# Spreading the column logits of a graph-attention layer without TensorE transposes, and ranking six last batches ahead instead of four

**Chip, cores, metric.** One core of one Trainium2 chip. The metric is the device time of one execution in microseconds (us); lower is better.

## The reference, cut to what matters

128 independent graphs of 128 nodes and 512 features go through four residual layers, each followed by a layernorm. All is float32. The change touches the attention of layer 1 alone:

```python
h = einsum('bnc,cf->bnf', x, W)
s1 = h @ a1                                   # one number for each node (row logit)
s2 = h @ a2                                   # one number for each node (column logit)
e  = leaky_relu(s1[:, :, None] + s2[:, None, :], 0.2) * adj
att = softmax(e, axis=2)
x  = layernorm(x + elu(att @ h + beta * h))   # ... layers 0, 2 and 3 cut
```

Rows of `e` lie on partitions. So `s1` is a scalar of each partition, but `s2` has to stand as a row of 128 numbers on *every* partition. It is computed as a column, one number on each partition. How it gets from column to row is the subject.

## The kernel before

The kernel writes each batch as a generator ("chain") that asks for engines. A small planner runs all chains, orders the requests by when it reckons they can start, then by rank, and so records one fixed order of instructions for each engine. The reckoned durations decide only the order; on the chip every engine runs its list strictly in that order.

```python
def use(self, engine, work, take=None, late=0.05, urgent=False): ...
    # work: time reckoned on the engine; late: from its end until the result is there

def at(self, r):                               # when a request could start, by the plan
    engine, _, take, _, _ = r["want"]
    t = max(r["ready"] + (MARGIN if engine == "PE" else 0.0), self.free.get(engine, 0.0))
    ...
def run(self):
    ...  # takes the request with the least (at, not urgent, rank, n)
         # self.now = r["ready"] = t + work + late
```

`MARGIN` is 1.0 us and is given to TensorE's requests alone. The attention, for a group of two batches:

```python
def attention1(gr, h):
    yield gr.logits[h]
    ...
    b0 = yield use("PE", 0.3, "tr", late=0.2, urgent=True)
    p = bank([P, 2, P], "tr")
    for i in range(2):
        nc.tensor.transpose(p[:, i, :], s[:, 2 * h + i, 1:2].to_broadcast([P, P]), ident)
    be = yield use("DVE", 2.1, "e", urgent=True)
    z = one.tile([P, 2, P], F32, name="z")
    for i in range(2):
        nc.vector.tensor_scalar(z..., p..., s[:, 2 * h + i, 0:1], None, op0=ALU.add)
    give(b0)
    e = buf([P, 2, P], "e")
    nc.vector.scalar_tensor_tensor(e, z, ALPHA, z, op0=ALU.mult, op1=ALU.max)
    ...  # times adj, maximum; exponentials on ScalarE; normalise, block turn
    yield use("SP", 0.1, late=2.0)
    to_rows(et..., scratch)                    # e_d <- et, and then eT <- e_d
    ...
# main: the last four batches rank 16 places ahead (in group() too)
for i in range(NB):
    plan.start(batch(i), i if i < NB - 4 else i - 16)
plan.run()
```

A transpose of a column broadcast along its free axis gives the row on every partition, in PSUM, in one step.

## Time and profile before

| | before |
|---|---|
| median (first three runs) | 3364.07 us (3363.28 to 3366.58) |
| profiled span | 3366.0 us |
| TensorE busy | 3324.6 us, 99% |
| VectorE busy | 2669.9 us, 79% |
| transposes of `s` | 128 records, source line 383 |
| TensorE's waits over 0.15 us, 20 to 3200 us | 9.5 us in all |
| the same from 3200 us to its last product | 16.5 us in all |

The last two rows are summed from TensorE's timeline, which gives the idle time before each group in brackets. I call these stretches "the middle" and "the end" below. The program is bound by TensorE nearly everywhere; the one large hole is near the end. The lines that carry this stand in the prediction.

How to read the names in profile lines: `out<-in` are tiles. `mm`, `tr` and `sc` are TensorE's results in PSUM. `x` is a batch, `xT` the batch turned for the query-key products of layer 3. `e`, `et` and `eT` are the attention matrix of layer 1, its block turn, and the turned copy that TensorE reads; `pr`, `pt` and `prT` are the same for layer 3. `scr` is the work tile of the products that make the logits `s`; names in `_d` are scratch in DRAM.

### The profile page before, as it was taken

The numbers are of one execution on the slowest core, as the hardware profiler recorded it, in microseconds if no ns is written. First come the engines' busy times: TensorE is split into PE (matmuls) and PEld (weight loads), VectorE is DVE, ScalarE is ACT, GpSimd is POOL, SyncE is SP. The second block draws the span as 40 slices with busy tenths as digits, with TensorE's granted clock in tenths as the row PEclk, the third lists the DMA queues.
The fourth block names the chain that finished last, engine by engine and source line by source line (L and its number), as shares of the span: only waits on it lengthen the run. The fifth ranks groups of instructions, "written<-read, shape, count | busy, mean of one in ns | idle before, by whom it ended". The sixth has DMA issues, their size and how long they took to land.

```text
span 3366.0 us, 43501 instructions
## 1 busy us (share of the span) xinstructions
PE 3324.6 (99%) x14729; PEld 2070.5 (62%) x14729; DVE 2669.9 (79%) x5527; ACT 1189.7 (35%) x3457; POOL 923.1 (27%) x1031
## 2 busy tenths in 40 slices
PE   9999999999999999999999999999999999999987
PEld 5665656566565666566656656665656665666655
DVE  7878786886978878877877886887887787788775
ACT  3433333333233334343333333333333333333332
POOL 2322221331322312312322331232232232232221
PEclk9999999999999999999999999999999999999999
DMA  4332323223232323222232322232322323232222
GB/s 157 98 103 63 104 75 93 69 80 113 68 99 76 97 79 91 94 79 82 79 109 66 100 85 91 85 89 83 91 85 82 98 73 97 76 94 88 69 82 75
DMA packets 458191, 296.01 MB, mean 88 GB/s; under 512 B 315888, under 2 KB 389744, under 8 KB 457968
## 3 DMA queue, kind: packets, MB, share of 16 engines
q1 hardware_dynamic: 457968, 293.23, 29.0%
q8 instruction: 117, 1.92, 0.2%
q14 instruction: 106, 0.87, 0.1%
HBM read 150.54 MB, written 142.61 MB: 87 GB/s over the span
## 4 chain that ended last, share of the span: by engine, by line
PE 90%; DVE 6%; DMA 2%; issue 1%; SPq 0%; ACT 0%; POOL 0%; POOLq 0%; DVEq 0%; ACTq 0%
PE mm L195 47%; PE mm L442 27%; PE tr L203 6%; PE sc L572 4%; PE tr L619 4%; PE mm L543 3%; DVE st L161 1%; DMA p_d<-pt 1%; DMA prT<-p_d 1%; DVE scr L516 1%; DVE x L648 1%; PE tr L383 0%; SPq L486 0%; DVE t L645 0%; DVE x L182 0%
## 5 line engine op out<-in xcount | busy, mean ns | idle before, releaser
L442 PE MATMUL mm<-xT,wqkv_sb 128*128 128x256 f32 x4096 | 918.2, 381 | 8.8 <-DVE st L161 8.8
L195 PE MATMUL mm<-w_sb,yT 128*128 128x512 f32 x2048 | 913.9, 596 | 2.3 <-ACT yT L206 2.3
L442 PEld LDWEIGHTS mm<-xT,wqkv_sb 128*128 128x128 f32 x4096 | 771.4, 190 | 138.3 <-issue 20.6
L168 POOL TENSOR_TENSOR rstd<-ve,neghalf 128x1 f32<-128x1 f32 x640 | 406.6, 635 | 1100.6 <-DVE ve L165 996.9
L195 PEld LDWEIGHTS mm<-w_sb,yT 128*128 128x128 f32 x2048 | 383.3, 191 | 453.3 <-issue 441.6
L188 POOL TENSOR_TENSOR x<-x,o 128x512 f32<-128x512 f32 x128 | 175.9, 1374 | 1128.3 <-DVE o L636 1117.6
L195 PE MATMUL mm<-wqkv_sb,xT 128*128 128x512 f32 x1024 | 464.4, 596 | 0.0
L195 PE MATMUL mm<-wproj_sb,oT 128*128 128x512 f32 x1024 | 460.9, 598 | 1.8 <-ACT oT L628 1.8
L590 ACT ACTIVATE pr<-pr,nmx 128x128 f32<-128x128 f32 x1024 | 397.6, 391 | 176.1 <-DVE nmx L586 174.6
L161 DVE BATCH_NORM_STATS2 st<-x 128x6 f32<-128x512 f32 x512 | 348.1, 680 | 3.1 <-ACT x L550 1.9
L579 DVE TENSOR_TENSOR pr<-sc,maskb 128x1024 f32<-128x1024 f32 x128 | 156.3, 1221 | 218.8 <-PE sc L572 218.0
L195 PEld LDWEIGHTS mm<-wproj_sb,oT 128*128 128x128 f32 x1024 | 191.8, 191 | 223.6 <-issue 214.4
L177 ACT ACTIVATE x<-x,nmr,rstd 128x512 f32<-128x512 f32 x256 | 205.0, 810 | 351.6 <-DVE nmr L175 326.9
L195 PEld LDWEIGHTS mm<-wqkv_sb,xT 128*128 128x128 f32 x1024 | 189.6, 190 | 199.0 <-issue 191.4
L206 ACT COPY yT<-tr 128x512 f32<-128x512 f32 x256 | 146.8, 582 | 263.9 <-PE tr L203 263.6
L188 POOL TENSOR_TENSOR x<-x,beta_sb 128x512 f32<-128x512 f32 x128 | 167.1, 1307 | 177.1 <-DVE xt L556 131.2
L516 DVE SCALAR_TENSOR_TENSOR scr<-x,wa_rows 128x512 f32<-128x512 f32 x256 | 200.4, 783 | 15.5 <-ACT x L177 10.2
L468 ACT COPY v<-mm 128x512 f32<-128x512 f32 x128 | 74.9, 585 | 347.7 <-PE mm L195 347.5
L450 ACT ACTIVATE qkT<-mm 128x512 f32<-128x512 f32 x128 | 76.1, 594 | 341.2 <-PE mm L442 341.0
L590 ACT ACTIVATION_READ_ACCUMULATOR pr<-pr,nmx 128x1 f32 x1024 | 193.1, 189 | 0.0
L188 POOL TENSOR_TENSOR x<-x,bias_sb 128x512 f32<-128x512 f32 x128 | 182.6, 1436 | 32.9 <-PE tr L203 22.9
L182 DVE TENSOR_SCALAR x<-x,mv,rstd 128x512 f32<-128x512 f32 x256 | 172.5, 676 | 14.4 <-POOL rstd L168 14.0
(63 smaller groups left out, 3558.6 us busy)
## 6 DMA issues: line engine op xcount, KB each, us to landing
p_d<-pt SPq DMA_DIRECT2D x128, 512.0 KB, 2.6
prT<-p_d SPq DMA_DIRECT2D x128, 512.0 KB, 3.8
x<-in_x SPq DMA_DIRECT2D x128, 256.0 KB, 2.9
x_d<-xt SPq DMA_DIRECT2D x128, 256.0 KB, 2.0
xT<-x_d SPq DMA_DIRECT2D x512, 64.0 KB, 2.5
out<-x SPq DMA_DIRECT2D x128, 256.0 KB, 2.0
e_d<-et SPq DMA_DIRECT2D x64, 128.0 KB, 1.7
eT<-e_d SPq DMA_DIRECT2D x64, 128.0 KB, 2.2
```

What stands on the lines that cost most here:

```text
L161: nc.vector.bn_stats(st, src)
L168: nc.gpsimd.tensor_tensor(rstd, ve, neghalf, op=ALU.pow)
L177: nc.scalar.activation(xb, xb, AF.Identity, bias=nmr, scale=rstd)
L182: nc.vector.tensor_scalar(xb, xb, mv[:, 0:1], rstd, op0=ALU.subtract, op1=ALU.mult)
L188: nc.gpsimd.tensor_tensor(dst, dst, other, op=ALU.add)
L195: nc.tensor.matmul(p, lhs(k), rhs(k), start=(k == 0), stop=(k == K - 1))
L203: nc.tensor.matmul(p[:, k, :], xb[:, k * P : (k + 1) * P], nodes, start=True, stop=True)
L206: nc.scalar.copy(yT, p)
L442: nc.tensor.matmul(p[:, j, :], wqkv_sb[:, k, (c + j) * P : (c + j + 1) * P], gr.xT[:, k, :], start=(k == 0), stop=(k == K - 1),)
L516: nc.vector.scalar_tensor_tensor(scr, xb, 1.0, wa_rows[:, j, :], op0=ALU.mult, op1=ALU.mult, accum_out=gr.s[:, b, j : j + 1],)
L579: nc.vector.tensor_tensor(pr, sc.rearrange("p j c m -> p (j c) m"), maskb[:, None, :].to_broadcast([P, H, P]), op=ALU.add,)
L590: nc.scalar.activation(pr[:, j, :], pr[:, j, :], AF.Exp, bias=nmx[:, j : j + 1], accum_out=sums[:, j : j + 1],)
```

## The change

The intent: TensorE is the bound, so take the 128 transposes from it. VectorE turns the column inside its 32x32 blocks, a 1 KB store writes the pieces to DRAM in node order, and a 128 KB load reads them back, the same row for every partition. Besides, six batches rank ahead instead of four, by 12 places instead of 16.

```diff
-        b0 = yield use("PE", 0.3, "tr", late=0.2, urgent=True)
-        p = bank([P, 2, P], "tr")
-        for i in range(2):
-            nc.tensor.transpose(p[:, i, :], s[:, 2 * h + i, 1:2].to_broadcast([P, P]), ident)
+        yield use("DVE", 0.2)
+        st = small.tile([P, 2, Q, S // Q], F32, name="s2")
+        nc.vector.transpose(
+            st.rearrange("p i c u -> p i u c"),
+            s[:, 2 * h : 2 * h + 2, 1:2, None].to_broadcast([P, 2, S // Q, Q]),
+        )
+        row = dram.tile([2 * Q, Q, S // Q], F32, name="s_d")
+        yield use("SP", 0.1, late=2.0)
+        nc.sync.dma_start(row..., st[::S]...)
+        bz = yield use("SP", 0.1, "z", late=2.2)
+        z = buf([P, 2, P], "z")
+        nc.sync.dma_start(z, row...[None, :].to_broadcast([P, 2 * P])...)
         be = yield use("DVE", 2.1, "e", urgent=True)
-        z = one.tile([P, 2, P], F32, name="z")
-        for i in range(2):
-            nc.vector.tensor_scalar(z..., p..., s[:, 2 * h + i, 0:1], None, op0=ALU.add)
-        give(b0)
+        nc.vector.tensor_tensor(
+            z, z, s[:, 2 * h : 2 * h + 2, 0:1].to_broadcast([P, 2, P]), op=ALU.add
+        )
         e = buf([P, 2, P], "e")
         nc.vector.scalar_tensor_tensor(e, z, ALPHA, z, op0=ALU.mult, op1=ALU.max)
+        give(bz)
...
-            plan.start(batch(i), i if i < NB - 4 else i - 16)
+            plan.start(batch(i), i if i < NB - 6 else i - 12)
```

(The ranks of `attention1` and `query_key` change in the same way. `z` gets two buffers.)

## The prediction

> **What bounds the kernel now.** I read the page first: the busy shares, then the chain that ended last. Both name TensorE.
>
> ```profile
> PE 3324.6 (99%) x14729; PEld 2070.5 (62%) x14729; DVE 2669.9 (79%) x5527; ACT 1189.7 (35%) x3457; POOL 923.1 (27%) x1031
> PEclk9999999999999999999999999999999999999999
> PE 90%; DVE 6%; DMA 2%; issue 1%; SPq 0%; ACT 0%; POOL 0%; POOLq 0%; DVEq 0%; ACTq 0%
> ```
>
> TensorE is busy 3324.6 of 3366.0 us, and its work is 90% of the chain. So only two things can shorten the span: less TensorE work, or fewer of the 41.4 us in which it idles. VectorE at 79% has room, and nothing that only it does counts unless TensorE waits for it.
>
> Then I looked for the idle time in the waits of TensorE alone:
>
> ```profile
> PE mm L442 <- DVE st L161: 8.8, 1, 8.8
> PE tr L619 <- DMA prT<-p_d: 7.9, 6, 6.0
> PE tr L383 <- DVE scr L516: 2.7, 4, 1.0
> PE tr L203 <- DMA eT<-e_d: 1.2, 1, 1.2
> ```
>
> The columns are microseconds in total, times, and the longest. One wait of 8.8 us is the largest; the second is one of 6.0 us and five small ones. The first transfers and the end of the program (the last matmul ends at 3356.9 of 3366.0, then VectorE and the store finish) make up most of the rest. Between 1000 and 3000 us the idle stretches I could find sum to only some 2 us. The timeline places the two long waits near the end:
>
> ```profile
> 3262.22 7.03 PE L195 MATMUL mm<-wproj_sb,oT 128*128 128x512 f32 x16
> 3278.04 16.80 PE L442 MATMUL mm<-xT,wqkv_sb 128*128 128x256 f32 x64 [8.79 <-DVE st L161]
> ...
> 3304.04 10.63 PE L442 MATMUL mm<-xT,wqkv_sb 128*128 128x256 f32 x48
> ...
> 3348.39 1.98 PE L619 MATMUL tr<-prT,v 128*64 128x128 f32 x16 [5.99 <-DMA prT<-p_d]
> ```
>
> The view blames a VectorE statistic for the 8.8 us, but that releaser is an inference. These products read xT; the last layer-2 product ended just before 3262.4, and after it come a maximum, an add, a layernorm, a block transpose and two steps of transfers. The four xT loads issued at 3273.42 took 2.55 us to issue and such a load lands in a median 2.5 us: that is the true releaser. There is a second loss: 64 records took 16.80 us here, though 48 took 10.63 us shortly after, which would be 14.2 us for 64. So 2.6 us more were lost to a slow clock after the pause.
>
> **What the Trainium skill says.** "TensorE: Matmul & The Clock Gate", Part 4 (PE-mode transpose), puts a transpose at about 275 ns inside a kernel. The trace agrees on duration (mean 281, median 273 ns), but duration is not what the engine loses: transposes are pipelined, and start to start tells the cost, below. The same page, Part 1 (the HAM clock gate), says that an idle window of some 3.4 us drops the clock to half; the trace agrees, both after the 8.79 us pause (above) and after the 5.99 us one (16 records in 1.98 us where the same group elsewhere takes 1.09). "DMA: Bandwidth & Descriptors", Anatomy of one DMA, gives about 2.0 us of fixed cost, mostly waiting for the write to be confirmed; the nearest transfers of this trace land in 1.7 us (store) and 2.2 us (load). "VectorE: DVE Perf Modes", The three transpose paths, says VectorE turns 32x32 blocks only, in 311 ns for 128x128; the trace has a mean of 311 ns for that shape. Hence blocks here need two transfers to become a row on every partition.
>
> **What the change removes.** 64 pairs of transposes (128 records). A pair costs what it delays its neighbours by:
>
> ```profile
> 1065.76 3.62 PE L442 MATMUL mm<-xT,wqkv_sb 128*128 128x256 f32 x16
> 1069.21 0.38 PE L383 MATMUL tr<-ident,s 128*128 128x128 f32 x2
> 1069.43 7.07 PE L442 MATMUL mm<-xT,wqkv_sb 128*128 128x256 f32 x32
> 1076.34 0.38 PE L383 MATMUL tr<-ident,s 128*128 128x128 f32 x2
> 1076.56 3.62 PE L442 MATMUL mm<-xT,wqkv_sb 128*128 128x256 f32 x16
> ```
>
> Start to start a pair takes 1069.43 - 1069.21 = 0.22 us, not 2 x 0.281. So 64 x 0.22 = 14.1 us of TensorE time go, all on the path, since TensorE runs gapless there. With them go TensorE's four direct waits for the logits, 2.7 us. These were transposes placed ahead of other work, just before VectorE had finished; I count them in full and keep an allowance below.
>
> **What it adds on VectorE.** Removed: the 128 adds that read the transposes from PSUM, 38.4 us in the rows by shape. Added: 64 block turns of 128x64. The trace has turns of 128 columns at 311 ns and of 512 at 702, so 1.02 ns a column, which gives an estimate of 0.25 us for 64: 16 us. And 64 adds of 128x256 SBUF operands; the like product with the adjacency takes 454 ns: 29.1 us. Sum 45 against 38.4: 7 us more on an engine with about 700 us free. No effect on the end.
>
> **What it adds in transfers.** 64 stores of 1 KB and 64 loads of 128 KB. By the nearest rows, the two together take some 0.3 + 1.7 + 0.4 + 2.2 = 4.6 us from turn to landing, against about one for the transposes. So a group's attention starts some 4 us later. This lies beside other work if the order is made for it: the recorded order of the new kernel places other products between. At the start, eleven batches of the first mix come ahead of the first product that needs attention in both orders, and one more layer-0 product now precedes it, so TensorE reaches it near 59.6 us (57.7 + 3.4 for the product - 0.6 for pairs - 0.9 for waits). I add up the new chain from the logits at 42.3 us: turn and add ahead of it 0.9, two transfers 4.6, four VectorE steps 1.8, exponentials 1.2, normalise and turn 2.0, two transfers 4.6: about 57.4 us. It fits by some 2 us.
>
> **What it moves.** The last six batches instead of four rank ahead, by 12 places instead of 16. In the old order, after the last layer-2 product only one pair of output projections is left to hide the road to xT: the 7.03 us group above, then the pause. In the new order there stand after it eight products of value mixing, two projections, eight more mixings, eight query-key products, eight mixings and two projections before the bulk of the last two groups' products. And the first of these groups seems to have its own layer-2 products over 40 us earlier (a group of 40 query-key products, some 17 us, stands between). So the 8.79 us pause and its 2.6 us of slow clock should go: 11.4 us. From the last 24 + 4 products of this stretch to the end the two orders are the same, so the 6.0 us wait for the last prT, its slow clock and the 9 us of finish should stay.
>
> **Sum.** 14.1 + 2.7 + 11.4 = 28.2 us. Against it an allowance of 3.2 us for new waits. It is a choice: SP issues in order and must wait 64 more times for a store to land before the load behind it, as it does today:
>
> ```profile
> SPq L216 <- DMA p_d<-pt: 258.2, 116, 4.5
> SPq L216 <- DMA e_d<-et: 69.3, 52, 2.1
> ```
>
> At the latter's 1.3 us a time that is some 85 us more of SP standing still, which can delay a prT behind it. Today TensorE's five short prT waits cost 1.9 us. Net 25 us: 3364.07 - 25 = **3339 us**, 0.74% faster, "same" at 2%.
>
> **The rivals.** (1) SP takes the place of TensorE's waits: the pairs of transfers stall loads of prT, xT and x, and TensorE waits a little in each of 64 groups. For it: SP's strict order, and five prT waits already at zero slack. Against it: SP waits over 600 us each for out and for pt to be produced, so it is mostly early. At 0.3 us a group this gives back 19 us: 3358. (2) The tail gap is not filled but moves, because the last groups still end their layer 2 together. For it: VectorE is dense near the end. Against it: the order above. It would leave only the transposes: 3348 to 3352. (3) VectorE becomes the bound where it is dense, in the first 60 us, and delays layer 0. The added 7 us over 3366 make this worth 2 us at most. (4) Everything works and the new order also trims the last prT wait and its cold products: 3331.
>
> **Range and chances.** The transposes are sure to within 1 us, the tail is a probable 11, the waits are open by some 10 either way. Low end: all of it plus a few us of the final wait, 3330. High end: the tail gain lost or SP costing some 15 us, 3353. To pass 2% would take 67 us, more than all idle time (41.4) and the transposes together (55.5), so faster has 0.01. Slower by 2% would need over 1 us of new wait per group: 0.01.
>
> **What would show it.** In the new profile: no transpose rows for s; TensorE's busy time near 3324.6 - 14.1 - 2.6 = 3308; no wait above 2 us of the query-key products near the end and the clock full until the last prT wait; that last wait still 4 to 8 us. The store lands in under 2.2 us, the load in under 2.6. VectorE's busy time rises by about 7 us. Waits for eT by TensorE stay under 3 us in all. I would be wrong if prT, eT or x waits in the middle sum to over 8 us (rival 1), if a pause of several us remains before query-key products near the end (rival 2), or if the first use of eT waits over 2 us.

## The result

| | before | after |
|---|---|---|
| median | 3365.32 us (4 runs) | 3353.43 us (3352.33 to 3360.93, 4 runs) |
| ratio | | 0.997 (0.9952 to 0.9987) |
| profiled span | 3366.0 us | 3351.8 us |
| TensorE's waits, middle / end | 9.5 / 16.5 us | 16.3 / 7.6 us |

12 us are gained by the medians, 0.35%, and 0.30% by the ratio. I had said 25, with 3330 us as the low end and 3353 as the high end; the median is just beyond the high end. The time is "same" at 2%, as forecast; the size is wrong by a factor of two.

First the page of the kernel after: busy time, and the chain that ended last.

```profile
PE 3312.7 (99%) x14601; PEld 2059.2 (61%) x14601; DVE 2664.7 (80%) x5527; ACT 1186.6 (35%) x3457; POOL 934.9 (28%) x1031
PE 85%; DVE 11%; DMA 3%; issue 1%; SPq 0%; ACT 0%; POOL 0%; POOLq 0%; DVEq 0%; ACTq 0%
```

TensorE's busy time fell by 11.9 us and its 128 records are gone. The shares of the chain tell more: TensorE's fell from 90% to 85%, VectorE's nearly doubled from 6% to 11%. More of the path now leads through VectorE, although VectorE is no busier than it was (2669.9 us before).

TensorE's waits after (us in total, times, longest):

```profile
PE tr L630 <- DMA prT<-p_d: 7.2, 3, 6.1
PE mm L554 <- ACT x L177: 3.9, 4, 2.0
PE sc L583 <- DVE qkT L463: 2.8, 3, 1.2
PE mm L195 <- DVE e L404: 2.7, 1, 2.7
PE mm L554 <- DVE x L520: 1.3, 1, 1.3
```

The 8.8 us pause before the query-key products is gone. The last prT wait, 6.1 us, is what it was. What is new is a scatter of waits for VectorE, or for ScalarE work that itself came after VectorE. (Not all of them hang on the new step: the wait of 2.7 us for `e`, at 843.6 us, stands with 2.68 us in e6 too, where nothing waits for z. It belongs to the new order.) Then VectorE's own side. It has this wait, the fourth largest of VectorE's, which the old kernel did not have at all:

```profile
DVE z L400 <- DMA z<-s_d: 60.8, 36, 4.1
```

In 36 of 64 groups VectorE stood still in front of the add that needs the new row, 1.7 us on average, with later work for other batches queued behind it. The chain in order of time (start us, us, what) shows one such stop all the way to TensorE:

```profile
2195.47 2.13 DMA s_d<-s
2197.62 3.01 DMA z<-s_d
2200.63 0.02 issue
2200.65 0.97 DVE z L400
2201.62 0.02 issue
2201.65 1.38 DVE e L404
...
2208.09 1.26 DVE e L425
...
2209.82 0.82 ACT x L177
2210.64 0.04 issue
2210.68 3.34 PE mm L554 x4
```

The store takes 2.13 us, the load 3.01, VectorE then works off its queue, and ScalarE comes last. TensorE paid for it, as its timeline shows (start us, us, group, and in brackets the idle time before it):

```profile
2205.04 3.62 PE L453 MATMUL mm<-xT,wqkv_sb 128*128 128x256 f32 x16
2210.68 3.34 PE L554 MATMUL mm<-x,adjT 128*128 128x512 f32 x4 [2.03 <-ACT x L177]
```

And the pause also cost clock. The windows view (stretch, length, busy time and records, granted clock, DMA share, GB/s):

```profile
2210.00:2215.00 5.00, 4.32 (x7) 0.66 0.21 56
2215.00:2220.00 5.00, 5.00 (x25) 1.00 0.03 8
```

### The profile page after: what moved, and what is told of

Same layout as the page of the kernel before. It is cut to its first block, busy times and chain, and to the rows that moved or that the text cites. A ratio compares the mean times of both kernels' runs of the same rounds, so it can differ in the third digit from the quotient of the medians.

```text
span 3351.8 us, 43540 instructions
## 1 busy us (share of the span) xinstructions
PE 3312.7 (99%) x14601; PEld 2059.2 (61%) x14601; DVE 2664.7 (80%) x5527; ACT 1186.6 (35%) x3457; POOL 934.9 (28%) x1031
## 4 chain that ended last, share of the span: by engine, by line
PE 85%; DVE 11%; DMA 3%; issue 1%; SPq 0%; ACT 0%; POOL 0%; POOLq 0%; DVEq 0%; ACTq 0%
PE mm L195 44%; PE mm L453 25%; PE tr L203 5%; PE sc L583 4%; PE tr L630 4%; PE mm L554 3%; DVE st L161 2%; DVE scr L527 1%; DMA z<-s_d 1%; DVE x L659 1%; DVE x L182 1%; DVE x L520 1%; DVE mv L163 0%; DVE t L656 0%; DMA s_d<-s 0%
## 5 line engine op out<-in xcount | busy, mean ns | idle before, releaser
L168 POOL TENSOR_TENSOR rstd<-ve,neghalf 128x1 f32<-128x1 f32 x640 | 413.8, 647 | 1285.2 <-DVE ve L165 1100.7
L182 DVE TENSOR_SCALAR x<-x,mv,rstd 128x512 f32<-128x512 f32 x256 | 161.5, 635 | 15.4 <-POOL rstd L168 14.6
L583 PEld LDWEIGHTS sc<-qkT 64*128 64x128 f32 x2048 | 124.8, 187 | 75.9 <-issue 60.3
```

The lines of the kernel that those rows point to most:

```text
L168: nc.gpsimd.tensor_tensor(rstd, ve, neghalf, op=ALU.pow)
L182: nc.vector.tensor_scalar(xb, xb, mv[:, 0:1], rstd, op0=ALU.subtract, op1=ALU.mult)
L583: nc.tensor.matmul(sc[:, j, c, :], gr.qkT[rws, c, nodes], gr.qkT[rws, K + c, nodes], start=True, stop=True,)
```

## The experiments

My theory after the result (A): the transposes were worth what I said, but VectorE, which runs its list in order, now stands in front of z, and the work queued behind it reaches TensorE late; that gives back what the transposes had saved. Rival B: the transposes were nearly free, so there was nothing to gain. Rival C: the new waits come from the order having been shuffled, or from SP, and not from z. Each time "before" is of the same chip job. VectorE's waits are those for z; the middle and the end are TensorE's waits as defined above, from one profile each.

| run | reckoned for store + load | VectorE's waits for z | middle / end | median, us | ratio to before |
|---|---|---|---|---|---|
| e0_after_again | 2.0 + 2.2 | 63.5 us, 41 times | 19.1 / 7.7 | 3357.54 | 0.9972 (0.9960 to 0.9985) |
| e1_rank_only | transposes kept | none | 11.3 / 6.5 | 3358.32 | 0.9968 (0.9954 to 0.9982) |
| e2_turn_only | 2.0 + 2.2 | 52.6, 36 | 16.9 / 9.2 | 3358.92 | 0.9977 (0.9965 to 0.9990) |
| e3_twice_transposed | transposes doubled | none | 9.2 / 16.3 | 3379.47 | 1.0039 (1.0026 to 1.0051) |
| e6_same_order_no_z_wait | 2.0 + 2.2, z unread | none | 9.5 / 7.7 | 3343.55 | 0.9932 (0.9920 to 0.9945) |
| e7_little_later_plan | 2.7 + 2.9 | 22.3, 13 | 12.0 / 6.5 | 3343.59 | 0.9932 (0.9919 to 0.9944) |
| e4_later_plan | 3.5 + 3.7 | 20.1, 11 | 11.8 / 7.4 | 3345.93 | 0.9936 (0.9924 to 0.9949) |
| e8_much_later_plan | 5.0 + 5.2 | 3.3, 3 | 4.5 / 8.1 | 3335.26 | 0.9907 (0.9892 to 0.9922) |
| e10_later_plan_old_ranks | 5.0 + 5.2 | 2.7, 3 | 3.4 / 16.5 | 3345.39 | 0.9938 (0.9926 to 0.9950) |
| e9_latest_plan | 6.5 + 6.7 | 0.4, 1 | 1.3 / 14.3 | 3337.27 | 0.9913 (0.9898 to 0.9928) |
| e11_latest_plan_eight_ahead | 6.5 + 6.7 | 1.9, 2 | 2.0 / 3.6 | 3327.39 | 0.9882 (0.9865 to 0.9898) |

All gave correct results but e6, which is wrong.

### The changed kernel again (e0_after_again)

No edit.

> The changed kernel unaltered, for the spread and as the partner of the others on this chip. All theories: some 12 us (0.3 to 0.4%) under the kernel before, near 3353 us; VectorE again stands about 60 us in some 36 waits for z; the waits of TensorE between 100 and 3200 us sum to about 15 us.

9 us under its before (12 in the first job); the two intervals overlap. It serves as the partner of e1, e2 and e4, which ran in the same job.

### The ranks alone, and the turn alone (e1_rank_only, e2_turn_only)

```diff
 # e1: the kernel before, with
-            plan.start(batch(i), i if i < NB - 4 else i - 16)
+            plan.start(batch(i), i if i < NB - 6 else i - 12)
 # e2: the kernel after, with
-            plan.start(batch(i), i if i < NB - 6 else i - 12)
+            plan.start(batch(i), i if i < NB - 4 else i - 16)
```

> The kernel before with only the ranks changed (last six batches, 12 places). If the 8.8 us pause and its slow clock were the rank's doing, they go: -11 us, 3354 us, ratio 0.9966, TensorE's waits in the middle as before (under 10 us). If the pause went only because attention and ranks were changed together, the pause stays and the ratio is 1.000.

> The changed kernel with the old ranks (last four batches, 16 places). Theory A (transposes are worth 14 us and their waits 3, but VectorE, waiting in order for z, gives about 10 back): -5 us and, as its order leaves a single projection to hide the road to xT, a pause of 10 to 12 us before the query-key products near the end, so 3358 to 3364 us, ratio 0.998 to 1.000; VectorE stands 50 to 70 us for z. Theory B (the transposes were nearly free): slower than before, over 3368 us.

The ranks alone give 8.6 us by the medians, 10.8 by the ratio, as expected: the end's waits fall from 16.5 to 6.5 us (the middle, 11.3 us, is a little over the 10 that I had named). That is all that the whole change gives (0.9968 against 0.9972). So in the form in which it came, the new way of spreading the logits gained nothing that these runs can resolve on top of the ranks.

For e2 I expected a pause of 10 to 12 us near the end. That was a miss: no such pause came, the end's waits fell to 9.2 us with the old ranks too. The old order had the pause; either part of the change draws a new order, and both new orders were without it. The gains of the two parts therefore don't add: each alone removes the same hole. The rest of e2 agrees with theory A: 52.6 us of waits for z, and TensorE's waits in the middle up from 9.5 to 16.9 us.

### What the transposes cost (e3_twice_transposed)

```diff
-        for i in range(2):
+        for i in (0, 1, 0, 1):
             nc.tensor.transpose(p[:, i, :], s[:, 2 * h + i, 1:2].to_broadcast([P, P]), ident)
```

> The kernel before with each pair of transposes done twice into the same bank, so 128 more records of 0.109 us on TensorE. If a pair costs 0.22 us of the span as worked out, +14 us, ratio 1.0042. If the transposes were nearly free (hidden in gaps that are there anyway), within 4 us of before, under 1.0012.

13.1 us for 128 more records, 0.20 us a pair. Worked out from start to start: 0.22. Rival B falls. The middle and the end are as before, so this is work alone.

### The same order, without VectorE's wait (e6_same_order_no_z_wait)

```diff
+        e = buf([P, 2, P], "e")
         nc.vector.tensor_tensor(
-            z, z, s[:, 2 * h : 2 * h + 2, 0:1].to_broadcast([P, 2, P]), op=ALU.add
+            e, maskb[:, None, :]..., s[:, 2 * h : 2 * h + 2, 0:1].to_broadcast([P, 2, P]), op=ALU.add
         )
-        e = buf([P, 2, P], "e")
-        nc.vector.scalar_tensor_tensor(e, z, ALPHA, z, op0=ALU.mult, op1=ALU.max)
+        nc.vector.scalar_tensor_tensor(e, e, ALPHA, e, op0=ALU.mult, op1=ALU.max)
```

The planner sees no data, so the recorded order of every engine is that of the changed kernel. Turn, store and load are all still there. Only the add reads a constant tile, so nothing waits for the load (the result is wrong, relative error 0.025).

> The changed kernel, wrong on purpose: every instruction of all engines in the same order and both transfers issued as before, but VectorE adds a constant tile instead of z, so that it never stands waiting for z. Theory A (VectorE's standing is what gives the gain back): 10 to 16 us under the changed kernel, 3340 to 3346 us, ratio 0.992 to 0.9945, TensorE's waits in the middle under 8 us. Theory C (the order by itself, or SP): within 4 us of the changed kernel, ratio 0.996 to 0.998.

The ratio falls from 0.9972 (e0, another job, so ratios are compared) to 0.9932, some 13 us, inside what theory A said and outside C's range; the two intervals don't touch. TensorE's waits in the middle came down to 9.5 us (not under 8 as I had said). This is the clearest run, for the order is the same to the instruction in the traces too, and SP does the same work: it waits 52.5 us in 52 stops for the stores, against 51.1 in 51, so e6 did not free SP as well. At the place shown above, TensorE's timeline of e6 reads (columns as before):

```profile
2202.88 1.88 PE L554 MATMUL mm<-x,adjT 128*128 128x512 f32 x4
2205.01 10.63 PE L453 MATMUL mm<-xT,wqkv_sb 128*128 128x256 f32 x48 [0.25 <-ACT qkT L461]
```

The same four products, without the pause of 2.03 us in front of them and in 1.88 us instead of 3.34, since the clock stayed full.

### Telling the plan the truth (e7_little_later_plan, e4_later_plan, e8_much_later_plan)

If VectorE stands because the plan put its steps too early, then a plan that reckons more for the transfers must cure it. Only two numbers change:

```diff
-        yield use("SP", 0.1, late=2.0)
+        yield use("SP", 0.1, late=3.5)           # e7: 2.7, e8: 5.0
-        bz = yield use("SP", 0.1, "z", late=2.2)
+        bz = yield use("SP", 0.1, "z", late=3.7) # e7: 2.9, e8: 5.2
```

> The changed kernel; the recording plan reckons 3.5 and 3.7 us for the two new transfers instead of 2.0 and 2.2, so that VectorE's four steps stand later in its order. Theory A (the time given back is VectorE standing in front of z): its waits for z fall from 61 to under 15 us, TensorE's waits in the middle from about 15 to under 9 us, the time to about 3343 us, ratio 0.9935. Theory C (the new waits come from the reshuffled order or from SP, not from z): z's waits fall but the time stays within 4 us of the changed kernel.

> The changed kernel with 2.7 and 2.9 us reckoned for the two transfers. Theory A: between the changed kernel (61 us of waits for z, ratio 0.9972) and the plan with 3.5 and 3.7 (20 us, 0.9936): some 40 us of waits for z and 0.995 to 0.9965. Theory C: no relation to z's waits; anything from 0.993 to 0.998.

> The changed kernel with 5.0 and 5.2 us reckoned. Theory A: waits for z under 8 us and a time as good as with 3.5 and 3.7 or a little better, 3340 to 3346 us, ratio 0.992 to 0.9945, unless the attention now comes too late and TensorE waits for eT by over 6 us. Theory C: no relation, 0.993 to 0.998.

e4 came out at 0.9936 where A said 0.9935, though with 20 us of waits for z left rather than 15, and 11.8 us of waits in the middle rather than under 9. Of these 11.8, 6.4 us in three stops were for eT, so there TensorE did wait for an attention that came late (0.6 us in the changed kernel). e7 was a miss in the good direction: 22 us of waits, not 40, and as fast as e4. Each plan draws another order, and a few us depend on what it draws; so e4 and e7 don't make a smooth curve. e8 is better than both, and better than I had said (0.992 to 0.9945). VectorE's waits for z in the three, in the order e7, e4, e8:

```profile
DVE z L400 <- DMA z<-s_d: 22.3, 13, 4.8
```

```profile
DVE z L400 <- DMA z<-s_d: 20.1, 11, 4.6
```

```profile
DVE z L400 <- DMA z<-s_d: 3.3, 3, 1.6
```

With 3.3 us left, TensorE's waits in the middle are 4.5 us, half of what the kernel before has, and the time is 31 us under before: more than I had predicted for the change. Not all of this is the missing wait: e6, with no wait for z at all in the order of the changed kernel, came to 0.9932 only. The other 0.0025, some 8 us, are of the order that e8's plan drew, and no run here takes them apart.

Why 4.2 us was too little can be read from the start times of the instructions. In the profile of the changed kernel the shortest way from the end of a turn to the start of its add was 4.52 us. In the 36 cases where VectorE stood waiting the median was 4.97 us, and a tenth took over 8.1. The plan had reckoned 4.45 (0.05 + 0.1 + 2.0 + 0.1 + 2.2). So no case is seen in which the reckoned time was enough, and nothing was kept for the times when SP was busy with something else: the store left 0.03 us after its turn in the median, but in a tenth of the groups 1.5 us or more after. The load could usually be issued 1.69 us after the store, sooner than the 2.1 of the plan; the load itself took 3.06 us in the median from its issue to the waiting add, where the plan had 2.3 and I had 2.6. The load is the term that both had too small.

### Which ranks (e10_later_plan_old_ranks, e9_latest_plan, e11_latest_plan_eight_ahead)

```diff
 # e10: e8 with the old ranks
-            plan.start(batch(i), i if i < NB - 6 else i - 12)
+            plan.start(batch(i), i if i < NB - 4 else i - 16)
 # e9: e8 with late=6.5 and late=6.7
 # e11: e9 with eight batches ahead
-            plan.start(batch(i), i if i < NB - 6 else i - 12)
+            plan.start(batch(i), i if i < NB - 8 else i - 12)
```

> 5.0 and 5.2 us reckoned, with the old ranks (last four batches, 16 places). If the ranks matter no more once the order is another (as with the old plan, where the turn alone also lost the pause), the ratio is within 0.0015 of 0.9907. If the new ranks are what removes the pause here, a pause of some 9 to 12 us stands before the query-key products near the end and the ratio is about 0.994.

> The changed kernel with 6.5 and 6.7 us reckoned for the two transfers. With 5.0 and 5.2 VectorE waited 3.3 us for z and the ratio was 0.9907; little is left to gain there, so within 4 us of that, 0.9895 to 0.992, unless the attention now comes late for TensorE, which its waits for eT would show.

> 6.5 and 6.7 us reckoned, and the last eight batches rank 12 places ahead, chosen because in the recorded order eight value products and more stand between the last scores and the last value mixings. With the last six, the middle had hardly a wait left but one of 12.8 us stood near the end. If the middle stays (under 3 us of waits) and the end loses most of that wait, 7 to 10 us under that kernel, about 3329 us, ratio 0.989; if the waits of the end only move, 3335 to 3338 us.

With the old ranks there is a hole near the end again, this time in front of a layer-2 product, and the ratio is 0.9938, as the second branch of the expectation had it:

```profile
PE mm L554 <- ACT x L177: 11.3, 4, 8.7
```

So the ranks do matter, but not by themselves: which batches must run ahead depends on the rest of the plan. e9 shows the same from the other side. Its middle is nearly free of waits (1.3 us), but its order ends badly and gives the gain back in one stop:

```profile
PE tr L630 <- DMA prT<-p_d: 12.8, 1, 12.8
```

e11 ranks eight batches ahead with that plan. Its waits are what is left when both are right:

```profile
PE tr L203 <- DMA x<-in_x: 3.2, 2, 1.8
PE tr L630 <- DMA prT<-p_d: 2.9, 3, 2.2
PE tr L308 <- DMA adj_sb<-in_adj: 2.6, 1, 2.6
```

The first and the third are the first transfers of the program. e11 takes 3327.39 us, 1.2% under the kernel before and 0.8% under the changed kernel (3353.43, another job). It beats both. I chose the eight by looking through recorded orders for one with other work in front of the last value mixings; the chip confirmed it in four timed executions (0.9882, where I had expected 0.989).

## Why the prediction was wrong

- **What bounds the kernel**: right. TensorE is the bound before and after, and removing its work or its waits is what counted in every run.
- **The transposes, 14.1 us**: right. Doubling them costs 13.1 us.
- **The pause and its slow clock, 11.4 us**: right in size (the ranks alone: 10.8 us by the ratio), only in part in cause. I put it down to the ranks. e1 shows that they suffice, e2 that they are not needed: it lost the pause with the old ranks, and e10 had another hole with them. It was a property of the order drawn. That the loads of xT end this pause, as I had read against the view, is what e3's profile says of it outright (8.7 us `<- DMA xT<-x_d`).
- **VectorE's added work, 7 us**: its terms were about right, the turn at 278 ns in the mean against my 250, the add at 486 against 454; together 48.9 us against the 38.4 removed, so 10.5 us and not 7. The engine's sum even fell by 5 us, because other steps ran shorter (the scaling `x<-x,mv,rstd` by 10 us). e6 keeps all this work and is 23 us under before, so little of the loss can hang on it, as I had said.

```profile
L383 DVE STREAM_TRANSPOSE s<-s 128x64 f32<-128x64 f32 x64 | 17.8, 278 | 0.0
L400 DVE TENSOR_TENSOR z<-z,s 128x256 f32<-128x256 f32 x64 | 31.1, 486 | 61.4 <-DMA z<-s_d 60.8
```

The last columns are what I had not thought to ask for: 31.1 us of work, and 61.4 us of standing in front of it.
- **The transfers, "This lies beside other work if the order is made for it"**: this is the step that failed, and with it the allowance of 3.2 us. The length was about right, 4.6 us estimated and 4.97 in the median where it was waited for. But I checked the order only for TensorE, in the first 60 us (where it came to the attention at 60.4 us without a wait; I had said 59.6) and near the end. The order was made for 4.45 us, and the steps stood on VectorE as soon as that had passed, without the margin that TensorE's requests get. VectorE is the engine that stood still. "TensorE: Matmul & The Clock Gate", Part 1 (the passage on queue depths under Architectural detail), says that ScalarE and VectorE are strictly first-in, first-out; this trace agrees, 60.8 us in 36 stops. An engine with 20% of its time free can't use it while it waits at the head of its list.
- **The sum**: 28.2 us gross, 11.9 measured, so 16.3 us came back. TensorE's waits in the middle went from 9.5 to 16.3 us while the 2.7 us of waits for transposes went away: 9.5 us of new waits. One more half-clock stretch, as after the pause of 2.03 us, adds some 1.7 us, an estimate from the granted clock above, (1 - 0.66) x 5 us. The transposes gave 1 us less than I had counted (13.1 by e3). Some 4 us I cannot assign, or 2 if the profiled spans are compared (3366.0 and 3351.8, so 14.2 gained). TensorE's waits shorter than 0.15 us are not it: they sum to 0.5 us before and 0.3 after. e6 says that some 13 of the 16 hang on VectorE's waiting for z.
- **The rivals**: rival 1 named a time near the measured one (3358) but the wrong waiter: prT waits in the middle are about 1 us in all. SP did wait for the new stores, 51.1 us in 51 stops, which I had estimated at 85, and TensorE hardly felt it directly. Rival 3 came nearest, VectorE as the one that is late, but I gave it 2 us because I counted its work and not its waiting. Rival 2 did not happen. Rival 4's 3331 us was reached only by another kernel, e11, with another plan and other ranks.
- **What would show it**: none of my three signs of being wrong came true. TensorE's waits for prT, eT and x in the middle were 1.6 us, no long pause stood before the last query-key products, and the first use of eT did not wait. All three look at TensorE and its transfers; a list with VectorE's waits for z would have found the cause at once. The signs that did fail were the load (3.06 us against "under 2.6"), TensorE's busy time (3312.7 against 3308) and VectorE's (5 us less, not 7 more).

## What to carry to other kernels

When a step moves from an engine to a transfer, ask which in-order engine will stand in front of the landed data, not only whether the data is late for the bound. A plan or a software pipeline that reckons the typical latency, without any slack, makes that engine stop in half of the cases (36 of 64 here). Reckoning 10.2 us for the two transfers instead of 4.2 was worth some 22 us here, of which 13 are shown to be the waiting (e6) and the rest came with another order; 7.2 us (e4) gave 12. And when a change redraws the whole order, measure each part alone: here two parts removed the same hole, and the one that the change was named for had gained nothing yet.

## What the Trainium skill lacked or had wrong

- "TensorE: Matmul & The Clock Gate", Part 1: it gives an idle window of about 3.4 us before the clock halves, and calls the window free-running; the table "Why this matters for your kernels" advises against pauses of over some 3 us. Here a pause of 2.03 us was enough (granted clock 0.66 from 2210 to 2215 us in the changed kernel), and one of 1.93 us in e4 (0.68 from 660 to 665 us), while in e0 a pause of 2.69 us, and in e4 one of 2.77, left it at 1.00. The clock records of the traces show what counts. The starts of the half-clock stretches of one profile lie whole multiples of 3.413 us apart (in the changed kernel 400.0, 728.0 and 733.0 of them after the first), so there is a fixed grid. I added up TensorE's idle time (gaps over 0.15 us) inside each cell of it, from 25 us to the last product in all thirteen profiles: every full-clock cell with 1.93 us or more of it, 26 in all, is followed by half clock, and none with 1.89 us or less is. So a pause that is split between two cells can be longer and cost nothing: of the 2.69 us in e0 at most 1.79 fell into one cell, while the same pause in the changed kernel, the same program, had 2.22 in one and lost the clock.
- The same page, Part 4: it gives the duration of a transpose, about 275 ns in a kernel, which this trace confirms (median 273), but not what one costs between other products. Start to start it is 0.11 us, and doubling them cost 0.10 us each.
- "DMA: Bandwidth & Descriptors", Anatomy of one DMA: it gives about 2.0 us of fixed cost for the transfers that GPSIMD issues. Those here are issued by SP; the store took a little less (the load behind it was issued after 1.69 us in the median). No page that I read gives a load that reads one row of 1 KB for all 128 partitions: 3.06 us in the median from issue to the waiting add.
- No page that I read says how much slack an order of instructions recorded ahead should keep for a transfer: 4.45 us reckoned, against 4.97 in the median and over 8.1 in a tenth of the cases that waited, cost 13 us here (e6).
